# The first head's keys and queries loaded as the last stage of the preparation

## The chip, the cores and the metric

The kernel runs on one core of a Trainium2 chip. The metric is the device time of one launch in microseconds (us). All times of single instructions below come from one profiled execution, and are given as microseconds from the start of its span.

## The reference

The program applies four layers to an input of 4 images of 128 channels by 64 x 64 pixels. Layers 0 and 1 are a state-space block and a convolution, layers 2 and 3 are attention layers with an expert feed-forward each. The change touches the attention of layer 2 alone, which sees an image as L = 4096 tokens of 128 features, that is 16 heads of 8 features:

```python
heads = x.reshape(Bs, Ss, H, D)                  # x is the normed input, H = 16, D = 8
qkv = _qz_ring(heads + rx_theta)                 # products of cosines
q = jnp.transpose(qkv, (0, 2, 1, 3))
scores = jnp.einsum('bhsd,bhtd->bhst', q, q) / np.sqrt(D)
attn = jax.nn.softmax(scores, axis=-1)
ctx = jnp.einsum('bhst,bhtd->bhsd', attn, q)
ctx = jnp.transpose(ctx, (0, 2, 1, 3)).reshape(Bs, Ss, Es)
attn_out = ctx @ w_comb.T + b_comb
x1 = _ln(x + attn_out, g1, beta1)
zf = jnp.cos(x1[..., :NQ_FFN]) * jnp.cos(ry_theta)
h = jax.nn.relu(zf @ w1.T + b1)
ffn_out = h @ w2.T + b2
return _ln(x1 + ffn_out, g2, beta2)              # added to the layer's input by the caller
```

Queries, keys and values are one and the same array q.

## The kernel before

`layer2_attention` runs over the four images b. Activations lie in DRAM (`xd[b]`, 128 features by 4096 tokens). An image has 8 chunks of 512 tokens (`CH`), 32 tiles of 128 tokens. For each b the kernel has two parts:

- **The mixed part.** `prepare(b)` and `feed_forward(b - 1)` are two generators, which `run` advances in turn, a stage each (`in_turns`, L757). Each is a software pipeline over the 8 chunks (`in_turn`, L747): `prepare` has the stages fetch, norm, products and store, `feed_forward` has fetch, attended, first_norm, cosines, hidden, sum_up and last_norm. `prepare` has 4 stages and `feed_forward` 7, so `prepare` runs out first. For b = 0 there is no feed-forward, and after the last image one feed-forward runs alone.
- **The attention.** `attention(b)` goes over the heads h and over blocks of 4 tiles, in steps. In each step PE makes the scores, ACT the exponentials `ex` (4 buffers of a pair of tiles each), DVE transposes (`turned`), POOL sums part of the exponentials (`folded`, `quarters`) and PE weighs the values (`ctx_ps`, `acc_ps`). The order on PE, DVE and POOL is the order in which the code writes it (`manual_schedule`). In the mixed part a scheduler decides the order. Every engine and every DMA queue works through its own list in order, so an entry that waits holds up all behind it.

In `prepare`, the stage `store` copies a chunk's q into `qt` (SBUF) and into `later`, from which `value_d` (DRAM) is written, two chunks at a time for the first three of four block rows. It transposes q, splits it into a high and a low part (`part`) and writes both to `head_d` (DRAM).

In `attention`, `load(h)` (L936) reads one head's keys and queries from `head_d`, 16 DMAs of 64 KB each for the keys and 16 for the queries. Keys read both halves of the tokens of a parity of tiles, queries those of a parity of chunks. `rounded` (L945) casts a loaded tile in place on POOL. The first head is loaded at the start of the attention, on two DMA queues (SP for keys, ACT for queries), and cast at once. The head after it is loaded, on SP alone, while the head before runs. `load_values` (L952) reads a block row's values (`v`, 4 DMAs of 32 KB each) and `spread_values` (L960) multiplies them into `turned_v` on POOL. At the start of the attention two block rows are read and spread.

In `feed_forward`, `fetch` reads a chunk's `den`, `num`, `nrm_in` and `x`; `last_norm` makes the second layer norm (its last instruction is the addition of beta on POOL into `blk`, L120), adds it to `x` on POOL (L1231) and stores to `xd` (L1232).

The pools decide which memory is free when. The mixed part's pool `l2_mid` and the attention's pool `l2_work` follow each other on the same memory, so a tile of the second waits until what lay there before is no longer in use:

```python
with tc.tile_pool(name="l2_big", bufs=1) as big:
    with (
        tc.tile_pool(name="l2_mid", bufs=2) as work,
        ...
    ):
        ...
        run(*parts)
    ...
    with (
        tc.tile_pool(name="l2_work", bufs=2) as work,
        ...
        attention(qt, past, big, work, pssc, psctx, psacc)
```

Of the kernel before, what the change touches and what calls it, by code (L numbers as in the profile page):

```python
# [9 lines left out]
F32 = mybir.dt.float32  # L10
F32R = mybir.dt.float32r
# [6 lines left out]
P = 128  # L18
NB = 4
HW = 64  # L20
L = HW * HW
CH = 512
NCH = L // CH
NTT = L // P
# [750 lines left out]
def layer2_attention(K, xd, dpool, w):  # L775

    nc, tc, mm = K.nc, K.tc, K.mm
# [4 lines left out]
    with ExitStack() as ctx:  # L782
# [50 lines left out]
        den_d = dpool.tile([2, NH, L], F32, name="den_d")  # L833
        nrm_d = [dpool.tile([P, L], F32, name=f"nrm_d{i}") for i in range(2)]

        def prepare(b, big, work, psum):

            n = NTT * NH * (HD + 1)  # L840
            qt = big.tile([P, n + 32], F32, name="qt")
            nc.gpsimd.memset(qt[:, n:], 0.0)
            values = qt[:, 0:n].rearrange("p (h t d) -> p t h d", h=NH, d=HD + 1)
            nc.gpsimd.memset(values[:, :, :, HD : HD + 1], 1.0)
            later = work.tile([P, NH, NTT, HD], F32, name="later", bufs=1)
            shape = [P, 4, NH, HD]
            heads, xs, nrms = {}, {}, {}

            def fetch(c):
                xs[c] = work.tile([P, CH], F32, name="x_in", bufs=3)  # L850
                nc.sync.dma_start(out=xs[c], in_=xd[b][:, c * CH : (c + 1) * CH])

            def norm(c):
                nrms[c] = work.tile([P, CH], F32, name="nrm", bufs=3)
                K.layernorm(nrms[c], xs.pop(c), work, psum)
                nc.sync.dma_start(out=nrm_d[b % 2][:, c * CH : (c + 1) * CH], in_=nrms[c])

            def products(c):

                tp = psum.tile([P, 4, P], F32, name="tok_t", tag="mm")  # L860
                for j in range(4):
                    nc.tensor.transpose(tp[:, j, :], nrms[c][:, j * P : (j + 1) * P], K.ident)
                phi = work.tile(shape, F32, name="phi")
                nc.vector.tensor_tensor(
                    phi.rearrange("p t h d -> p (t h) d"),
                    tp.rearrange("p j (h d) -> p (j h) d", d=HD),
                    theta.unsqueeze(1).to_broadcast([P, 4 * NH, HD]),
                    ALU.add,
                )
                cs = heads[c] = work.tile(shape, F32, name="cs", bufs=3)  # L870
                K.cos(cs, phi, work, shape, "cos")
                cc = lambda d: cs[:, :, :, d : d + 1].rearrange("p t h o -> p (t h) o")
                q0 = work.tile([P, 4 * NH, 1], F32, name="q0")
                nc.gpsimd.tensor_tensor(q0, cc(1), cc(2), ALU.mult)
                for d in range(3, HD):
                    nc.gpsimd.tensor_tensor(q0, q0, cc(d), ALU.mult)
                for d in range(1, HD):
                    nc.vector.tensor_tensor(cc(d), cc(d - 1), cc(d), ALU.mult)
                nc.vector.tensor_copy(cc(0), q0)

            def store(c):

                cs = heads[c]
                nc.scalar.copy(values[:, 4 * c : 4 * c + 4, :, 0:HD], cs)
                nc.gpsimd.tensor_copy(later[:, :, 4 * c : 4 * c + 4].rearrange("p h t d -> p t h d"), cs)
                j = c // 2
                if c % 2 and j < NJ - 1:
                    for q in range(4):
                        nc.sync.dma_start(
                            out=value_d[:, :, j, q].rearrange("h s t d -> s h (t d)"),  # L890
                            in_=later[32 * q : 32 * q + 32, :, BT * j : BT * j + BT].rearrange("s h t d -> s h (t d)"),
                        )
                tp = psum.tile([P, 4, P], F32, name="q_t", tag="mm")
                for j in range(4):
                    nc.tensor.transpose(tp[:, j, :], cs[:, j].rearrange("p h d -> p (h d)"), K.ident)
                tq = work.tile([P, CH], F32, name="tq", tag="phi")
                nc.scalar.copy(tq, tp.rearrange("p j t -> p (j t)"))
                rest = work.tile([P, CH], F32, name="rest", tag="cos_r")
                nc.vector.scalar_tensor_tensor(rest, tq, 4097.0, tq, ALU.mult, ALU.subtract)
                part = work.tile([P, 2, CH], F32, name="part")  # L900
                nc.vector.scalar_tensor_tensor(part[:, 0], tq, 4097.0, rest, ALU.mult, ALU.subtract)
                nc.gpsimd.tensor_tensor(part[:, 1], tq, part[:, 0], ALU.subtract)
                nc.sync.dma_start(
                    out=head_d[:, :, c * CH : (c + 1) * CH].rearrange("z q s -> q z s"), in_=part
                )

            return in_turn(NCH, fetch, norm, products, store), qt

        def attention(qt, dsum, big, work, pssc, psctx, psacc):

# [1 line left out]

            unit = lambda p, c: slice(32 * (2 * p + c), 32 * (2 * p + c) + 32)
            dacc = big.tile([P, NJ - 1, NH, NTT], F32, name="dacc")
            nc.gpsimd.memset(dacc, 0.0)

            def load(h, queues=(nc.sync, nc.sync)):

                out = []
                for keys in (True, False):
                    t = work.tile([P, L // 2], F32R, name="keys" if keys else "queries")
                    raw = t.bitcast(F32)
                    n = P if keys else CH
                    for p in range(2):  # L930
                        for c in range(2):
                            for k in range(4):
                                r = unit(p, c).start + HD * k
                                src = head_d[k // 2 if keys else k % 2, HD * h : HD * h + HD]
                                at = p if keys else c
                                queues[not keys].dma_start(  # L936
                                    out=raw[r : r + HD].rearrange("d (m s) -> d m s", s=n),
                                    in_=src.rearrange("d (m z s) -> d m z s", z=2, s=n)[:, :, at],
                                )
                    out.append(t)  # L940
                return out

            def rounded(t):

                nc.gpsimd.tensor_copy(t, t.bitcast(F32))  # L945

            def load_values(h, j):

# [31 lines left out]
            for n, (h, j, _) in enumerate(steps):  # L980
                begins.setdefault((h, j), n)
                last[h, j] = n
            heads = {0: load(0, (nc.sync, nc.scalar))}
            for t in heads[0]:
                rounded(t)
            values = {(0, 0): spread_values(load_values(0, 0))}
            waiting = []
            order = [(h, j) for h in range(NH) for j in range(NJ - 1)]
# [114 lines left out]
            for n, (h, j, m) in enumerate(steps):  # L1103
                now[0] = n
                keys, queries = heads[h]
                if j in (1, 2) and h + 1 < NH:
                    at = n - begins[h, 1]
                    if at == 0:
                        heads[h + 1] = load(h + 1)
                    if at in (11, 15):  # L1110
                        rounded(heads[h + 1][at == 15])
                while waiting and n >= waiting[0][0]:
# [48 lines left out]
        def feed_forward(b, dsum, work, psum):  # L1161
# [3 lines left out]
            def fetch(c):  # L1165
# [4 lines left out]
                nc.sync.dma_start(out=num, in_=num_d[:, :, cols].rearrange("p q f -> q p f"))  # L1170
                nrm = work.tile([P, CH], F32, name="nrm_in", bufs=4)
                nc.sync.dma_start(out=nrm, in_=nrm_d[b % 2][:, cols])
                x = work.tile([P, CH], F32, name="x", bufs=8)
                nc.sync.dma_start(out=x, in_=xd[b][:, cols])
                loads[c] = x, num, den, nrm

            def attended(c):
                _, num, den, at = loads[c]

                tp = psum.tile([P, 4, 2 * NH], F32, name="den_t", tag="mm")  # L1180
                for j in range(4):
# [15 lines left out]

            def first_norm(c):
                x1 = x1s[c] = work.tile([P, CH], F32, name="x1", bufs=4)
                K.layernorm(x1, loads[c][3], work, psum, g1, beta1)  # L1200

            def cosines(c):
                zp = psum.tile([P, CH], F32, name="z_ps", tag="mm")
# [13 lines left out]
                    nc.scalar.activation(hid[:, k, :], hps[k], AF.Relu, bias=b1[:, k : k + 1])  # L1217

            def sum_up(c):
                hid = hids[c]  # L1220
                fp = psum.tile([P, CH], F32, name="ffn_ps", tag="mm")
                for k in range(4):
                    mm(fp, w2T[:, k, :], hid[:, k, :], start=k == 0, stop=k == 3)
                r = sums[c] = work.tile([P, CH], F32, name="res")
                nc.vector.scalar_tensor_tensor(r, fp, b2, x1s[c], ALU.add, ALU.add)

            def last_norm(c):
                o = work.tile([P, CH], F32, name="blk")
                K.layernorm(o, sums[c], work, psum, g2, beta2)
                x = loads[c][0]  # L1230
                nc.gpsimd.tensor_tensor(x, x, o, ALU.add)  # L1231
                nc.sync.dma_start(out=xd[b][:, c * CH : (c + 1) * CH], in_=x)  # L1232

# [1 line left out]

        past = None
        for b in range(NB + 1):
            with tc.tile_pool(name="l2_big", bufs=1) as big:
                with (
                    tc.tile_pool(name="l2_mid", bufs=2) as work,  # L1240
                    tc.tile_pool(name="l2_ps", bufs=8, space=PSUM) as psum,
                ):
                    parts = [feed_forward(b - 1, past, work, psum)] if b > 0 else []
                    if b < NB:
                        part, qt = prepare(b, big, work, psum)
                        parts.append(part)
                    run(*parts)
                if b == NB:
# [2 lines left out]
                with (  # L1251
# [5 lines left out]
                        engines={mybir.EngineType.PE, mybir.EngineType.DVE, mybir.EngineType.Pool}  # L1257
                    ),
                ):
                    attention(qt, past, big, work, pssc, psctx, psacc)  # L1260


def expert_ffn(K, xs, w, tag):
# [430 lines left out]
```

## Time and profile before

| | us |
|---|---|
| median of 3 runs | 11169.24 (11165.61 to 11181.6) |
| the profiled execution, by the same measure | 11175.99 |
| its span | 11174.1 |

| busy over the span | PE | DVE | ACT | POOL |
|---|---|---|---|---|
| us | 9093.3 | 7817.5 | 7349.5 | 6136.5 |
| share | 81% | 70% | 66% | 55% |

The span falls into layers 0 and 1 (to about 3240), layer 2's attention block (to about 10025, four mixed parts and four attentions, and a last feed-forward) and the rest. Of layer 2 the parts look alike from the second image on:

| stretch | start to end |
|---|---|
| preparation of image 0 | 3235 to 3359 |
| attention of image 0 | 3398 to 4774 |
| feed-forward of 0 with preparation of 1 | 4775 to 5043 |
| attention of image 1 | 5086 to 6460 |
| feed-forward of 1 with preparation of 2 | 6460 to 6730 |
| attention of image 2 | 6772 to 8147 |
| feed-forward of 2 with preparation of 3 | 8147 to 8416 |
| attention of image 3 | 8459 to 9830 |
| feed-forward of 3 | 9830 to 10018 |

How to read the rows of the profile: a group has its line, engine and operation, then output<-input, shapes and count, then busy time and mean duration in ns, then the idle time of the engine just before these instructions with what ended most of it. A row of the timeline has start and duration in us, then engine, line, operation and count, and in brackets the idle time before it and its releaser; neighbouring instructions of one kind are drawn together, so a duration with a count above one spans gaps too. SPq and ACTq are the two DMA queues; their rows tell when transfers are issued, not when they land.

### The profile page before, as it was taken

The numbers are of one execution on the slowest core, as the hardware profiler recorded it, in microseconds if no ns is written. First come the engines' busy times: TensorE is split into PE (matmuls) and PEld (weight loads), VectorE is DVE, ScalarE is ACT, GpSimd is POOL, SyncE is SP. The second block draws the span as 40 slices with busy tenths as digits, with TensorE's granted clock in tenths as the row PEclk, the third lists the DMA queues.
The fourth block names the chain that finished last, engine by engine and source line by source line (L and its number), as shares of the span: only waits on it lengthen the run. The fifth ranks groups of instructions, "written<-read, shape, count | busy, mean of one in ns | idle before, by whom it ended". The sixth has DMA issues, their size and how long they took to land.

```text
span 11174.1 us, 183363 instructions
## 1 busy us (share of the span) xinstructions
PE 9093.3 (81%) x71376; PEld 3383.0 (30%) x71376; DVE 7817.5 (70%) x8718; ACT 7349.5 (66%) x9690; POOL 6136.5 (55%) x3631
## 2 busy tenths in 40 slices
PE   5777777778757999967999967999967999966767
PEld 2222223223122333322333322333322333323433
DVE  2688687687846788856888756878856888844564
ACT  2655454654527899947988947988946998842431
POOL 0466455455626777726777736777736777720000
PEclk8787878878778999978999979999978999978888
DMA  3322322322212221122221222221122221122004
GB/s 86 83 70 52 100 64 62 92 62 61 61 46 39 34 33 34 30 73 36 37 33 32 32 74 34 38 32 33 32 73 34 35 37 33 32 87 78 30 16 136
DMA packets 524324, 581.53 MB, mean 52 GB/s; under 512 B 106232, under 2 KB 329536, under 8 KB 520896
## 3 DMA queue, kind: packets, MB, share of 16 engines
q1 hardware_dynamic: 520896, 565.61, 22.4%
q8 instruction: 563, 9.22, 0.4%
q10 hardware_dynamic: 2560, 4.20, 0.3%
q14 instruction: 305, 2.50, 0.1%
HBM read 373.96 MB, written 76.55 MB: 40 GB/s over the span
## 4 chain that ended last, share of the span: by engine, by line
PE 35%; DVE 16%; DMA 8%; SPq 4%; ACT 3%; issue 2%; POOL 1%; DVEq 0%; ACTq 0%; POOLq 0%
PE ctx_ps L89 12%; PE acc_ps L89 9%; DVE turned L1129 5%; PE score L89 5%; DVE turned L1148 5%; SPq L936 4%; DMA queries<-head_d 3%; DMA keys<-head_d 2%; PE ln_var L89 2%; PE ln_xc L89 1%; PE hid_ps L89 1%; DMA w<-in_L_ffn_weight 1%; PE ffn_ps L89 1%; ACT ex L1142 1%; PE kv L89 1%
## 5 line engine op out<-in xcount | busy, mean ns | idle before, releaser
L1142 ACT ACTIVATE ex<-score 128x1024 f32<-128x1024 f32 x5120 | 4904.7, 1031 | 598.5 <-PE score L89 224.9
L1090 POOL TENSOR_TENSOR folded<-ex 128x1024 f32<-128x1024 f32 x960 | 2291.5, 2387 | 1173.3 <-ACT ex L1142 1141.8
L89 PE MATMUL ctx_ps<-ex,qt 128*32 128x512 f32 x20480 | 2722.5, 596 | 0.0
L1148 DVE STREAM_TRANSPOSE turned<-ex 128x1024 f32<-128x1024 f32 x1536 | 1892.0, 1232 | 596.5 <-ACT ex L1142 392.8
L89 PE MATMUL acc_ps<-turned,turned_v 128*32 128x256 f32 x24576 | 1828.5, 389 | 220.7 <-DVE turned L1129 219.0
L1129 DVE STREAM_TRANSPOSE turned<-ex 128x1024 f32<-128x1024 f32 x1536 | 1854.8, 1208 | 0.0
L89 PE MATMUL score<-queries,keys 32*128 32x512 f32 x10240 | 1360.2, 497 | 240.9 <-POOL queries L945 145.9
L641 DVE TENSOR_TENSOR_SCAN hs<-decay,carry,hs 128x512 f32<-128x512 f32 x1024 | 1247.8, 1263 | 151.6 <-ACT decay L640 142.3
L640 ACT ACTIVATE decay<-dt,a_neg 128x512 f32<-128x512 f32 x1024 | 699.9, 690 | 875.1 <-DVE hs L641 871.5
L1091 POOL TENSOR_TENSOR quarters<-folded 128x512 f32<-128x512 f32 x960 | 1233.8, 1285 | 75.3
L647 POOL TENSOR_TENSOR hs<-hs,c_sb 128x1024 f32<-128x1024 f32 x512 | 1201.7, 2368 | 48.1 <-DMA c_sb<-c_d 28.4
L89 PEld LDWEIGHTS score<-queries,keys 32*128 32x128 f32 x10240 | 523.4, 182 | 2300.9 <-issue 1656.8
L89 PEld LDWEIGHTS acc_ps<-turned,turned_v 128*32 128x32 f32 x24576 | 562.1, 108 | 938.9 <-issue 545.2
L89 PE MATMUL y_ps<-hs,pair 128*64 128x512 f32 x2048 | 654.5, 757 | 223.0 <-POOL hs L647 222.8
L89 PEld LDWEIGHTS ctx_ps<-ex,qt 128*32 128x32 f32 x20480 | 684.9, 110 | 462.2 <-DVE ctx L1072 53.2
L637 DVE TENSOR_TENSOR hs<-dtx,b_ps 128x2048 f32<-128x2048 f32 x256 | 581.4, 2271 | 318.9 <-PE b_ps L89 218.2
L644 POOL COPY carry<-hs 128x4 f32<-128x4 f32 x256 | 65.1, 254 | 1105.2 <-DVE hs L641 1090.8
L1135 DVE TENSOR_REDUCE dacc<-quarters 128x2 f32<-128x512 f32 x960 | 617.2, 648 | 0.0
L1072 DVE COPY ctx<-ctx_ps 128x512 f32<-128x512 f32 x256 | 177.1, 692 | 565.3 <-PE ctx_ps L89 565.3
L89 PE MATMUL ln_var<-ln_sq,mean 128*128 128x512 f32 x448 | 289.6, 732 | 219.0 <-ACT ln_sq L104 183.1
L89 PE MATMUL b_ps<-dbc,spread 32*128 32x512 f32 x512 | 341.6, 751 | 147.8 <-DVE hs L637 147.8
L960 POOL TENSOR_TENSOR turned_v<-v,quarter 128x1024 f32<-128x1024 f32 x192 | 458.9, 2391 | 0.0
(344 smaller groups left out, 9320.8 us busy)
## 6 DMA issues: line engine op xcount, KB each, us to landing
c_sb<-c_d SPq DMA_DIRECT2D x512, 128.0 KB
keys<-head_d SPq DMA_DIRECT2D x1024, 64.0 KB
queries<-head_d SPq DMA_DIRECT2D x960, 64.0 KB
dt<-dt SPq DMA_DIRECT2D x128, 256.0 KB
dtx<-dtx SPq DMA_DIRECT2D x128, 256.0 KB
w<-in_L_ffn_weight SPq DMA_DIRECT2D x32, 1024.0 KB
w<-in_L_ffn_weight SPq DMA_DIRECT2D x128, 256.0 KB
under<-xp SPq DMA_DIRECT2D x384, 66.0 KB
```

The source lines that it names most:

```text
L89: self.nc.tensor.matmul(out, lhsT, rhs, start=start, stop=stop)
L637: nc.vector.tensor_tensor(hs, dtx2, bb.unsqueeze(1).to_broadcast([P, NQ, CH]), ALU.mult)
L640: nc.scalar.activation(ex, dt2[:, q, :], AF.Exp, scale=a_neg[:, q, g : g + 1])
L641: nc.vector.tensor_tensor_scan(hs[:, q, :], ex, hs[:, q, :], carry[:, g, q : q + 1], ALU.mult, ALU.add)
L647: nc.gpsimd.tensor_tensor(at, at, cs.unsqueeze(1).to_broadcast([P, 2, CH]), ALU.mult)
L960: nc.gpsimd.tensor_tensor(t, v.unsqueeze(2).to_broadcast([P, 4 * BT, 4, HD]), quarter.unsqueeze(1).to_broadcast([P, 4 * BT, 4, HD]), ALU.mult,
L1090: nc.gpsimd.tensor_tensor(hs, exs[:, :, 0], exs[:, :, 1], ALU.add)
L1091: nc.gpsimd.tensor_tensor(qs, hs[:, :, 0 : CH // 2], hs[:, :, CH // 2 :], ALU.add)
L1129: nc.vector.transpose(*upright)
L1135: nc.vector.tensor_reduce(at, qs, AX.X, ALU.add)
L1142: nc.scalar.activation(ex, sps[p], AF.Exp, scale=scale, accum_out=dacc[:, j, h, t : t + 1] if summed else None)
L1148: nc.vector.transpose(*upright)
```

## The change

- `load` and `rounded` move out of `attention`, and take the pool as an argument. All loads are now issued on SP.
- A pool `l2_two` of two buffers is opened beside `l2_big`, ahead of `l2_mid`; keys and queries of all heads are allocated in it.
- `prepare` gets a last stage, behind its pipeline: it loads head 0 and casts it. The mixed part's scheduler orders these instructions. `attention` receives the loaded head.
- To make room in `l2_mid`, `later` holds two chunks rather than all eight (one buffer), and its copies of the last two chunks, which nothing read, are left out. `x` of the feed-forward has 3 buffers for 8, and is read in `sum_up`, one stage ahead of its use, rather than in `fetch`.

```diff
-        def prepare(b, big, work, psum):
+        def load(h, keep_in):
+            out = []
+            for keys in (True, False):
+                t = keep_in.tile([P, L // 2], F32R, name="keys" if keys else "queries")
...
+                            nc.sync.dma_start(
...
+        def prepare(b, big, two, work, psum):
...
-            later = work.tile([P, NH, NTT, HD], F32, name="later", bufs=1)
...
-                nc.gpsimd.tensor_copy(later[:, :, 4 * c : 4 * c + 4].rearrange("p h t d -> p t h d"), cs)
                 j = c // 2
+                if c % 2 == 0 and j < NJ - 1:
+                    laters[j] = work.tile([P, NH, BT, HD], F32, name="later", bufs=1)
+                if j < NJ - 1:
+                    at = laters[j][:, :, 4 * (c % 2) : 4 * (c % 2) + 4]
+                    nc.gpsimd.tensor_copy(at.rearrange("p h t d -> p t h d"), cs)
...
-            return in_turn(NCH, fetch, norm, products, store), qt
+            first = []
+
+            def stages():
+                yield from in_turn(NCH, fetch, norm, products, store)
+                first.extend(load(0, two))
+                for t in first:
+                    rounded(t)
+                yield
+
+            return stages(), qt, first
...
-                    t = work.tile([P, L // 2], F32R, name="keys" if keys else "queries")
...
-            heads = {0: load(0, (nc.sync, nc.scalar))}
-            for t in heads[0]:
-                rounded(t)
+            heads = {0: first}
...
-                        heads[h + 1] = load(h + 1)
+                        heads[h + 1] = load(h + 1, two)
...
-                x = work.tile([P, CH], F32, name="x", bufs=8)
-                nc.sync.dma_start(out=x, in_=xd[b][:, cols])
-                loads[c] = x, num, den, nrm
+                loads[c] = num, den, nrm
...
             def sum_up(c):
+                x = loads[c] = work.tile([P, CH], F32, name="x", bufs=3)
+                nc.sync.dma_start(out=x, in_=xd[b][:, c * CH : (c + 1) * CH])
...
-            with tc.tile_pool(name="l2_big", bufs=1) as big:
+            with (
+                tc.tile_pool(name="l2_big", bufs=1) as big,
+                tc.tile_pool(name="l2_two", bufs=2) as two,
+            ):
```

## The prediction

> **What bounds the kernel now.** I read the page's groups first, for who waits, then the table of stretches over layer 2, then the timeline at one boundary. In the groups (busy, mean ns of one, then idle time before and its releaser) the score matmuls own a wait that no later matmul has:
>
> ```profile
> L89 PE MATMUL score<-queries,keys 32*128 32x512 f32 x10240 | 1360.2, 497 | 240.9 <-POOL queries L945 145.9
> ```
>
> The table of stretches (start:end, length, busy time of PE, PEld, DVE, ACT, POOL, granted clock, DMA share, GB/s) shows where it falls:
>
> ```profile
> 3360.00:3400.00 40.00, 1.80 (x6) 1.17 (x6) 0.00 (x0) 1.87 (x2) 5.59 (x3) 0.50 0.53 76
> 3400.00:4775.00 1375.00, 1302.10 (x14589) 464.53 (x14586) 1104.48 (x1169) 1230.01 (x1568) 1046.18 (x561) 1.00 0.20 32
> 4775.00:5045.00 270.00, 163.12 (x416) 71.61 (x416) 146.53 (x288) 115.27 (x171) 80.44 (x98) 0.75 0.25 78
> 5045.00:5088.00 43.00, 1.68 (x6) 1.16 (x6) 0.00 (x0) 1.74 (x2) 5.46 (x3) 0.50 0.53 61
> ```
>
> Attention (1375 us) holds PE busy 95% of it; a microsecond lost at its start has nothing to be recovered from later. Before each attention stand some 40 us in which no compute engine works. The timeline of the second boundary (start, length, engine, line) says what fills it:
>
> ```profile
> 5042.23 1.26 POOL L1231 TENSOR_TENSOR x<-x,blk 128x512 f32<-128x512 f32 x1
> 5045.59 28.35 SPq L936 DMA_DIRECT2D keys<-head_d  x16
> 5045.61 29.44 ACTq L936 DMA_DIRECT2D queries<-head_d  x16
> 5075.08 1.28 ACT L1142 ACT_TABLE_LOAD   x1 [36.49 <-DMA keys<-head_d]
> 5076.58 7.37 SPq L952 DMA_DIRECT2D v<-value_d  x8
> 5082.54 1.89 POOL L945 CAST keys<-keys 128x2048 fp32r<-128x2048 f32 x1 [39.05 <-DMA keys<-head_d]
> 5084.37 1.90 POOL L945 CAST queries<-queries 128x2048 fp32r<-128x2048 f32 x1
> 5086.23 4.68 POOL L960 TENSOR_TENSOR turned_v<-v,quarter 128x1024 f32<-128x1024 f32 x2
> ...
> 5087.54 3.77 ACT L1142 ACTIVATE ex<-score 128x1024 f32<-128x1024 f32 x4 [11.18 <-PE score L89]
> ...
> 5090.86 2.38 POOL L1090 TENSOR_TENSOR folded<-ex 128x1024 f32<-128x1024 f32 x1
> ```
>
> The feed-forward's last addition ends at 5043.49, its store lands about 2.1 us later and frees the pool, and only then do the 32 loads start, since their tiles lie in a pool on the same memory. They land 37 us later, are cast, and the first exponential runs 44.05 us after the feed-forward's end (43.50 and 44.03 at the third and fourth boundary: 6729.67 to 6773.17, 8415.85 to 8459.88). The data was ready long before: the last head_d store is issued by 4962.7, the first of the last six xd stores at 4981:
>
> ```profile
> 4948.05 14.69 SPq L903 DMA_DIRECT2D head_d<-part  x2
> 4980.99 62.84 SPq L1232 DMA_DIRECT2D xd<-x  x6
> ```
>
> **What the skill says.** The Trainium skill, *DMA: Bandwidth & Descriptors*, "Issuing engines are not separate DMA queues": issuing on two engines saves only sequencer time. The trace agrees: 32 loads on two queues took 29.5 us to issue, and those of head 1 on SP alone 11.18 + 14.70 = 25.9. The same page, "Anatomy of one DMA": a semaphore wait sits on the issuing sequencer, and a fixed cost of about 2 us is mostly the receipt; here last addition to first load is 2.1, 2.4 and 2.1 us. Its "Rules for kernel authors" advise an early DMA with a late wait, which is what the new placing is. *ScalarE: Activation LUTs*, "What ACT_TABLE_LOAD costs", gives 1283 ns; the trace shows 1.28 us, at present hidden behind the loads.
>
> **The change, part by part.** In the order of the built programs PE and DVE stand as before, instruction for instruction, and ACT too, but that it loses its 64 DMA issues. Only SP and POOL change. On POOL, second boundary, the end of the feed-forward reads:
>
> ```
> x+=blk (chunk 4); cast keys; blk 5; blk 6; cast queries; x+=blk 5; blk 7; x+=blk 6; x+=blk 7; turned_v x2; folded
> ```
>
> *1. The loads, moved to SP.* 3 wait for the even chunks alone and go ahead of the last head_d store; 1 + 16 + 12 follow it, then three xd stores, and x loads. Store at 4962.4 plus 2.6 us (3359.5 to 3362.1 at the first boundary) gives 4965; 16 keys at 0.70 us and 13 queries at 0.92 (head 1's pace) make 23.2 us, so 4988 for the last issue and, 7.4 us after (first boundary: last key load issued 3387.0, cast 3394.4), 4996 for landing. The keys' cast has its place at 5016.8, behind the addition of chunk 4: 21 us of room. Cover: the feed-forward's last five chunks. Cost 0; if the cover goes, one for one.
>
> *2. What SP queues behind them.* The xd store of chunk 2 is ready at 4981 and goes at 4988; no engine waits for it but x's load of chunk 5. That and chunks 6 and 7 wait for the stores of chunks 2, 3, 4; the last is made at 5016.8, lands by 5019, the loads by about 5023. Chunk 5's addition is at 5029. Cost 0, room 6 us. The slot waits of chunks 3 and 4 (2.1 us each) hold SP while its next entry, a head_d or nrm_d store, is not due: 0; at worst 2 x 2.1 x 3 boundaries = 13 us.
>
> *3. The casts on POOL.* Keys: in a 10.9 us idle stretch, 0. Queries (1.90): ahead of chunk 5's addition, from 5034.9 on, pushing the last addition from 5043.49 to 5044.66: 1.17 us each.
>
> *4. The new start.* Score matmuls need only PSUM, free by about 5041. The exponentials' buffers lie on the old pool, so ACT's table load waits for the last xd store to land: 5044.66 + 2.1 + 1.28 = 5048.1 against 5087.54. Gains: 44.05 - 4.55 = 39.5; 43.50 - 4.84 = 38.7; 44.03 - 4.55 = 39.5. **Sum 117.7 us.**
>
> *5. What is late next: the values.* The v loads are still in attention's pool: issued from about 5045.5, eight in 3.4 us (0.42 the median) to 7.4 (at this boundary), landed about 2.3 us after; two multiplications of 2.35 on POOL, in front of the first fold. Fold starts 6.3 to 9.8 us after the first exponential, against 3.3 now. Four ex buffers let ACT run on; at the first boundary an exponential waits for a fold only from the ninth pair (0.35 us), so there is about 1 us of slack: loss 2 to 5.3, I take 3.5 each: **-10.5.** POOL has some room in these steps (two folds of 3.67 us in four steps of 2.29), so the lag dies out, but PE's lost time stays.
>
> *6. The first boundary* has no feed-forward to hide under. 30 loads follow the last head_d store: 16 x 0.70 + 14 x 0.92 = 24.1 us from 3362.1, landed by 3392.6 to 3393.6, one cast left of two: score at 3394.6 instead of 3398.2. **+3.6** (0 to 7).
>
> *7. x's loads moved out of the start* of four feed-forwards: three of 256 KB (0.45 us of SP each) no longer stand among the first loads. **+4** in all (-4 to +8). *8. `later`* loses its copies of the last two chunks (2 x 0.61 us of POOL, beside idle time) and gets one buffer of two chunks, whose next use is 13 us or more after its stores are issued: 0. Head 1 and later load as before.
>
> Sum: 117.7 - 10.5 + 3.6 + 4 = 114.8 us. The profiled execution took 11175.99 (span 11174.1), so 11061 by its measure; the median of the runs, 11169.24, lies 6.8 lower, and 11169.24 - 114.8 = **11054.5, say 11055**.
>
> **The rivals.** *A: the values take the wait over.* If v lands as late after issue as the keys do (7.4 us) with the issues at 7.4, folds start 16 us after the exponentials and some 12 are lost each time: gain 89, 11080. For it: v goes on a queue full of head 1's keys. Against: the v loads stand ahead of most of them. *B: nothing is gained*, since the new pool's tiles or the exponentials wait for something I don't see: 11165. Against: the order has no such wait. *C, slower: the casts hold the feed-forward up.* Chunks 5 to 7 stand behind the queries' cast; loads that land after 5035 delay the end one for one. The gain of 39 is gone at 5077 (2.5 us of idle POOL before chunk 7's blk are used up first), 112 us after their start, that is 2.1 MB at 19 GB/s. Were only 16 GB/s left to them, 131 us, they would land at 5096 and the exponentials start at 5107, 19 us later than now: three times that, 58, with part 5's 10.5 and less the 7.6 of parts 6 and 7, is 61, and 11230. Against: the stretch moves 78 GB/s at a DMA share of 0.25, and alone the loads get 61 GB/s.
>
> **How the numbers follow.** 0.2% (22 us) is about what can be told from no change. As summed 0.76, own range 11040 to 11072; A 0.16; B 0.03; C 0.05. Faster 0.92, same 0.03, slower 0.05. The low end takes parts 5, 6, 7 at their best (loss 6, +7, +8: gain 127) and a few us for the boundary, 11037; the high end takes in A and 12 us of SP waits beside it, 11096.
>
> **What would show it.** Right: head 0's loads lie inside the feed-forward, landing 20 us before the keys' cast; ACT's table load about 3 us after the last addition; first exponentials near 5048 on this clock, shifted by the first boundary; the stretches of feed-forward still 270 us, those of attention about 1378. Wrong in part 1 or 2: POOL waits for queries or x inside the feed-forward, which grows past 272. Wrong in part 5: folds over 10 us behind the first exponential. The prediction fails if less than 75 us is gained.

## The result, and the profile after

| us | before | after |
|---|---|---|
| median | 11175.07 (11165.61 to 11181.6, 4 runs, three of them those above) | 11057.91 (11046.44 to 11065.94, 4 runs) |
| profiled execution, its span | 11175.99, 11174.1 | 11065.94, 11064.2 |

The ratio is 0.9896 [0.988, 0.9912], that is 116 us less (98 to 134); the changed kernel is about 1% faster. The prediction was 11055 (11037 to 11096).

In the page's groups the row of the score matmuls (columns as before) has lost the wait that it was chosen for: 124.5 us of idle time instead of 240.9, and POOL's cast of the queries no longer ends most of it (it still does at the first boundary, 40 us).

```profile
L89 PE MATMUL score<-queries,keys 32*128 32x512 f32 x10240 | 1358.8, 497 | 124.5 <-ACT ex L1153 74.7
```

The table of stretches of the changed kernel, with the first boundary, the first attention, the second mixed part and the second boundary:

```profile
3369.00:3408.00 39.00, 1.58 (x6) 1.07 (x6) 0.00 (x0) 1.67 (x2) 6.66 (x4) 0.50 0.53 77
3408.00:4778.00 1370.00, 1300.69 (x14568) 463.56 (x14572) 1101.20 (x1167) 1230.21 (x1568) 1044.76 (x557) 1.00 0.20 32
4778.00:5050.50 272.50, 163.93 (x444) 72.43 (x436) 149.70 (x290) 115.12 (x171) 83.36 (x99) 0.76 0.30 85
5050.50:5054.00 3.50, 0.00 (x0) 0.00 (x0) 0.00 (x0) 1.28 (x1) 0.00 (x0) 0.50 0.37 122
```

The second boundary is 3.5 us long where 43 us stood, and holds nothing but ACT's table load. The mixed part in front of it moves 85 GB/s at a DMA share of 0.30, instead of 78 at 0.25: the head's loads are in there now. The first boundary is as long as ever. The timeline of the second boundary, the answer to the prediction's:

```profile
4971.31 11.08 SPq L853 DMA_DIRECT2D keys<-head_d  x16
4982.65 10.82 SPq L853 DMA_DIRECT2D queries<-head_d  x12
4993.70 29.09 SPq L1243 DMA_DIRECT2D xd<-x  x3
...
5022.38 1.89 POOL L862 CAST keys<-keys 128x2048 fp32r<-128x2048 f32 x1
5023.60 1.37 SPq L1230 DMA_DIRECT2D x<-xd  x3
...
5040.54 1.89 POOL L862 CAST queries<-queries 128x2048 fp32r<-128x2048 f32 x1
5042.39 1.26 POOL L1242 TENSOR_TENSOR x<-x,blk 128x512 f32<-128x512 f32 x1
...
5047.84 2.48 POOL L1242 TENSOR_TENSOR x<-x,blk 128x512 f32<-128x512 f32 x2
...
5052.48 3.57 SPq L965 DMA_DIRECT2D v<-value_d  x8
5052.71 1.28 ACT L1153 ACT_TABLE_LOAD   x1 [8.46 <-DMA xd<-x]
5054.00 3.77 ACT L1153 ACTIVATE ex<-score 128x1024 f32<-128x1024 f32 x4
...
5055.81 4.70 POOL L973 TENSOR_TENSOR turned_v<-v,quarter 128x1024 f32<-128x1024 f32 x2 [5.50 <-DMA v<-value_d]
5060.47 2.38 POOL L1101 TENSOR_TENSOR folded<-ex 128x1024 f32<-128x1024 f32 x1
```

The last load is issued at 4982.65 + 10.82 = 4993.47, 29 us ahead of the keys' cast. Neither cast has a bracket, so POOL waits for no load. The bracket of the table load says that ACT waits for the feed-forward's last store, which is the prediction's part 4. The bracket of `turned_v` says that the values are what is late next, its part 5.

The ledger, from the same events in both traces (the first layer-2 load of `x_in`, the last addition to `part`, first and last exponential, last addition to `x`):

| us | before | after | difference |
|---|---|---|---|
| preparation of image 0, and from there to the first exponential | 123.39 + 40.32 | 123.79 + 39.08 | -0.84 |
| last addition to first exponential, boundaries 2 to 4 | 44.05, 43.50, 44.03 | 3.68, 3.56, 3.68 | -120.66 |
| three mixed parts | 274.49, 271.78, 275.15 | 272.64, 271.90, 273.18 | -3.70 |
| last feed-forward | 186.30 | 188.83 | +2.53 |
| four attentions | 1369.59, 1370.35, 1367.53, 1370.29 | 1370.07, 1369.96, 1368.16, 1369.83 | +0.26 |
| layer 2 | 6780.77 | 6658.36 | -122.4 |
| the rest of the span | | | +12.4 |

The rest is code that the change doesn't touch: layer 2 began at 3235.70 before, at 3244.74 after, and at anything from 3230.55 to 3248.60 in the experiments. So kernels are compared below by layer 2 and its parts. Two executions of the changed kernel differed by 14 us in layer 2 (6658.36 and 6644.36), spread over all its parts but the three later boundaries, which repeat to 0.1 us. A part's few microseconds in one execution are therefore no finding, unless they repeat at each boundary. This holds above all for experiments 3 to 8, which were executed once each.

### The profile page after: what moved, and what is told of

Read it like the earlier page. It is cut to its first block, busy times and chain, and to the rows that moved or that the text cites. A ratio compares the mean times of both kernels' runs of the same rounds, so it can differ in the third digit from the quotient of the medians.

```text
span 11064.2 us, 183405 instructions
## 1 busy us (share of the span) xinstructions
PE 9097.1 (82%) x71376; PEld 3379.2 (31%) x71376; DVE 7816.5 (71%) x8718; ACT 7349.4 (66%) x9690; POOL 6134.3 (55%) x3623
## 3 DMA queue, kind: packets, MB, share of 16 engines
q1 hardware_dynamic: 523456, 569.81, 22.2%
## 5 line engine op out<-in xcount | busy, mean ns | idle before, releaser
L89 PE MATMUL score<-queries,keys 32*128 32x512 f32 x10240 | 1358.8, 497 | 124.5 <-ACT ex L1153 74.7
```

What stands on the lines that cost most here:

```text
L89: self.nc.tensor.matmul(out, lhsT, rhs, start=start, stop=stop)
```

## The experiments

**1. The room alone.** The kernel before with the small `later` and the late `x`, but head 0 loaded in the attention, on two queues.

```diff
# against the kernel before
-            later = work.tile([P, NH, NTT, HD], F32, name="later", bufs=1)
+                    laters[j] = work.tile([P, NH, BT, HD], F32, name="later", bufs=1)
...
-                x = work.tile([P, CH], F32, name="x", bufs=8)          # in fetch
+                x = loads[c] = work.tile([P, CH], F32, name="x", bufs=3)   # in sum_up
```

> The kernel before, with only the edits that make room: later of two chunks, x with 3 buffers read in sum_up. My theory: the gain is the three hidden loads, and the room is worth nothing by itself. The boundaries keep their 43.5 to 44.1 us from last addition to first exponential, the mixed parts change by -1 to -3 us each (x is no longer among the first loads), the last feed-forward by +-2.5; total within 10 us of before, ratio 0.999 to 1.001. Rival: part of the 117 us gained comes from x's later reads, by 20 us or more: ratio 0.998 or below.

Measured: 11174.64 (12 runs) beside 11170.56 (15 runs of the kernel before), ratio 1.0002 [0.9994, 1.0011]. The later boundaries stay at 44.19, 41.45 and 44.47. The room itself brings nothing that 12 runs show (the interval is -7 to +12 us); the gain is the loads' place.

**2. The pool alone.** The changed kernel, but the loads and casts are written where `attention` begins, into the early pool.

```diff
                 yield from in_turn(NCH, fetch, norm, products, store)
-                first.extend(load(0, two))
-                for t in first:
-                    rounded(t)
                 yield
...
-            heads = {0: first}
+            heads = {0: load(0, two)}
+            for t in heads[0]:
+                rounded(t)
```

> The changed kernel, but head 0's loads and casts are written where they were, at the start of the attention; the pool still opens early. The scheduler can then move the loads up, since no memory holds them back, but places them behind the feed-forward's own transfers: in the built order 16 keys and 5 queries stand between the xd stores, and the last 7 queries behind the last of them. Theory A (the queue's order counts): those 7 are issued at about the time of the last store and land some 12 us later, the queries' cast follows, and each of the three boundaries has its first exponential 10 to 13 us later than in the changed kernel, so 14 to 17 us after the last addition instead of 3.7; total about 11094. Theory B (the pool alone counts, where the stage is written is nothing): 11058. Theory C (the early stage alone counts): as before, 11175.

Measured: 11083.67 (11070.69 to 11093.62, 4 runs), ratio 0.9918 [0.9901, 0.9935]; boundaries of 13.76, 14.03 and 13.62. The scheduler does move the loads into the feed-forward once their tiles are free, though the code has them later: three quarters of the gain come with the pool, without the stage (90 of 121 us at the three boundaries). What is left lies in SP's order, as the timeline of its second boundary shows:

```profile
5046.92 0.33 SPq L1242 DMA_DIRECT2D xd<-x  x1
5047.29 4.82 SPq L853 DMA_DIRECT2D queries<-head_d  x7
5052.28 4.18 SPq L962 DMA_DIRECT2D v<-value_d  x8
5056.30 1.89 POOL L862 CAST queries<-queries 128x2048 fp32r<-128x2048 f32 x1 [9.40 <-DMA v<-value_d]
```

Seven of the queries' loads stand behind the feed-forward's last store on the in-order queue, and the cast waits until 5056.30 (the release is put down to v, but the cast reads the queries, whose last issue was at about 5052.1). The stage in `prepare` is what ranks them ahead of the stores.

**3. Three times the loads.** Each of head 0's 32 loads is made three times, into the same tile.

```diff
-                for p in range(2):
+                for p in [p for _ in range(times) for p in range(2)]:
...
-                first.extend(load(0, two))
+                first.extend(load(0, two, 3))
```

> The changed kernel with head 0 loaded three times over into the same tiles, 96 DMAs for 32, to find how much the feed-forward hides. At the first boundary, with no cover, the 64 more cost their full time, 64 x 0.80 = 51 us. At the other three they land at about 5052 on the changed kernel's clock instead of 5001; the queries' cast stands ahead of the last three additions on POOL, where it now runs at 5040.5, and the xd stores and x loads stand behind the loads on SP. Theory (cover of 39 us, then one for one): the last addition ends 9 to 12 us later, and so does the first exponential: 41 of 51 us are hidden each time, total near 11058 + 51 + 30 = 11139. Rival (the added transfers disturb the feed-forward as they run, so nothing is really free): the mixed parts grow by 25 us or more each, total over 11185.

Measured: 11109.73. At the first boundary, where nothing covers them, the 64 further loads cost 45.3 us (84.42 for 39.08). In the mixed parts they cost +4.9, -0.2 and +5.6 (277.54, 271.70, 278.77), less than the 9 to 12 of the theory, and the boundaries stay at 3.70, 3.57, 3.70. In the timeline of its second mixed part:

```profile
5006.37 42.78 SPq L853 DMA_DIRECT2D keys<-head_d  x48
5049.45 32.28 SPq L853 DMA_DIRECT2D queries<-head_d  x44
...
5075.48 1.89 POOL L862 CAST keys<-keys 128x2048 fp32r<-128x2048 f32 x1
5084.66 1.90 POOL L862 CAST queries<-queries 128x2048 fp32r<-128x2048 f32 x1 [7.29 <-DMA xd<-x]
```

These 92 loads of 64 KB took 75.4 us to issue beside the feed-forward (5006.37 to 5081.73), 80 GB/s. Alone, at the first boundary, 93 took 73.5 us (3364.88 to 3438.39), 83 GB/s. Rival C needed 19 GB/s or less beside the feed-forward; the runs give four times that. Most of three times the traffic is covered, and here the cover ends: POOL waits 7.29 us ahead of the queries' cast, whose last load is issued at 5081.73 (the release is put down to the store of `x`). In this build the keys' cast also stands later in POOL's order, behind `blk` of chunks 5 and 6, so the cover isn't measured in an unaltered order.

**4. Later folds.** The first two multiplications of the values are made four times, or twice, so that POOL reaches the first fold later.

```diff
-                nc.gpsimd.tensor_tensor(t, ...)
+                for _ in range(times):
+                    nc.gpsimd.tensor_tensor(t, ...)
...
-            values = {(0, 0): spread_values(load_values(0, 0))}
+            values = {(0, 0): spread_values(load_values(0, 0), 4)}    # or 2; and for order[1]
```

> The changed kernel with the two multiplications of values at the start of each attention done four times each, 6 more of 2.35 us, so 14.1 us more of POOL ahead of the first fold. The prediction's rule (an exponential waits for a fold as soon as the lag passes about 1 us): the first copy of ctx_ps, which stands 38.9 us after the first exponential in the changed kernel, moves by about 14 us, and so does the attention's end: 4 x 14 = 56 us in all. What the trace of the changed kernel hints (3.2 us of lag moved that copy by -0.7 us, and before ACT idled 2.8 and 0.8 us at 28 to 31 us): some 4 to 6 us of the lag are absorbed within the first block, the rest counts: the copy moves by 8 to 10 us, the total by 32 to 40.

> The changed kernel with the first two multiplications of the values made twice instead of four times, so that the first fold is some 4.7 us later instead of 14.6: at the three later boundaries some 11.2 us after the first exponential. The prediction's rule (each microsecond of lateness past about 1 holds up the exponentials) says that each attention is 4.7 longer, 19 in all: 11077. The rule read from four times (up to some 7.7 us cost nothing, then one for one) says that the first ctx copy comes some 42.4 after the first exponential and each later attention is 3.5 longer, the first one (fold at 6.8) unchanged: some 10 to 11 in all, 11068. If the free lateness is larger than 11 at any boundary, nothing is seen there.

Measured, from the first exponential to the first fold (the lag) and to the first ctx copy, attention 0 and then the mean of attentions 1 to 3:

| us | lag | first ctx copy | length of the attention |
|---|---|---|---|
| after | 2.10; 6.59 | 39.15; 39.04 | 1370.07; 1369.32 |
| twice | 7.00; 11.42 | 42.80; 42.69 | 1372.10; 1371.94 |
| four times | 16.73; 21.19 | 52.61; 52.41 | 1383.36; 1383.01 |

At boundaries 2 to 4 a lag of 11.42 costs 3.65 up to the first ctx copy, and one of 21.19 costs 13.37: in both the first 7.8 us are free, and the rest counts one for one. At the first boundary 7.00 costs 3.65 and 16.73 costs 13.46: there only 3.3 us are free. The expectation for twice took attention 0 to have the room of the others, and missed there. (The times were 11052.61 for twice and 11087.45 for four times; layer 2 took 6661.90 and 6696.12.) ACT's timeline with four times says where the room lies, at the first boundary and then at the second:

```profile
3402.63 1.94 ACT L1154 ACTIVATE ex<-score 128x1024 f32<-128x1024 f32 x2 [0.47 <-PE score L89]
3414.47 1.94 ACT L1154 ACTIVATE ex<-score 128x1024 f32<-128x1024 f32 x2 [9.89 <-POOL folded L1102]
...
5058.55 5.61 ACT L1154 ACTIVATE ex<-score 128x1024 f32<-128x1024 f32 x6 [0.17 <-PE score L89]
5075.06 1.02 ACT L1154 ACTIVATE ex<-score 128x1024 f32<-128x1024 f32 x1 [10.91 <-POOL folded L1102]
```

At the first boundary ACT runs 8 exponentials, four steps, before it waits for a fold; at the second it runs 12, six steps. Two steps at 2.3 us are about the 4.5 us between 3.3 and 7.8. A step is two exponentials, and there are four buffers of a step each in both cases; what differs is which exponential has to wait. By the code the first, second, fifth and sixth step are folded, the third and fourth are not. At the first boundary the 9th and 11th exponential (steps 5 and 6) wait for the first and the second fold. At the second the 13th and 15th do (steps 7 and 8; their waits are 10.91 and 1.67), and with twice the 11th (2.83). That fits buffers that aren't handed out in turn: there step 5, or steps 5 and 6, take those of steps 3 and 4, which no fold reads. The traces hold no addresses, so this is inferred.

The changed kernel has an assignment of its own. In its third attention, at a lag of 6.76, it is the 9th exponential that waits:

```profile
6708.59 4.84 ACT L1153 ACTIVATE ex<-score 128x1024 f32<-128x1024 f32 x5 [0.23 <-POOL folded L1101]
```

So about 6.5 us are free in the changed kernel's later attentions (6.76 less 0.23, an estimate), and its lag just fits; the 7.8 belongs to kernels whose folds are later. At boundaries 2 to 4 the first exponential that waits for a fold is a later one in the builds with later folds: the 9th at a lag of 6.76, the 11th at 11.31, the 13th at 21.11. At the first boundary it is the 9th even at 16.73. Why the builds differ so isn't shown.

**5. Earlier values.** The first two blocks of values are loaded in the preparation's last stage, into the early pool, which the later blocks use too; the multiplications stay.

```diff
+                for at in ((0, 0), (0, 1)):
+                    first.append(load_values(*at, two))
                 yield
```

> The changed kernel with the first two block rows' value loads also issued in the preparation's last stage, into the early pool; their multiplications stay at the attention's start. The first fold then stands some 3 us after the first exponential at boundaries two to four, as before the change, instead of 6.5. The prediction's part 5 (10.5 us lost to late values): each attention ends 3.5 us sooner against its first exponential, 10.5 us in all. What spread_4 showed (a lag of up to some 7.7 us costs nothing at these boundaries, then one for one): first ctx copy 38.9 to 39.2 us after the first exponential as it is, attention 1370, gain 0.

Measured: 11059.23. The lag falls from 6.5 to 3.2 at the later boundaries, and the attentions last 1369.22, 1369.73, 1369.25 and 1369.71, as before. Part 5's wait is real, and costs nothing that shows.

**6. The table ahead of time.** An exponential of one column on the last chunk of the feed-forward (and of image 0's preparation), so that ACT's table is there when the buffers come free.

```diff
+                if c == NCH - 1:
+                    tiny = work.tile([P, 1], F32, name="tiny", bufs=1)
+                    nc.scalar.activation(tiny, o[:, 0:1], AF.Exp)
                 nc.gpsimd.tensor_tensor(x, x, o, ALU.add)
```

> The changed kernel with one exponential of a single column behind the last layer norm of each feed-forward, and behind the last chunk of image 0's preparation, so that ACT's table is loaded while the last store lands or the loads run. Theory: the table load now waits for what the exponential waits for, and adds its 1.28 us to each boundary. Expected: from last addition to first exponential 2.4 us instead of 3.7, first boundary 37.8 instead of 39.1 (give or take the 5 us by which its loads differ from run to run); layer 2 shorter by 5 us. Rival: the table load overlaps the wait for the store in hardware anyway, or ACT is not what the first exponential waits for: nothing changes.

Measured: 11039.76; boundaries of 2.41, 2.29 and 2.40, so 1.28 us less at each. In its timeline the first exponential now waits for the store directly:

```profile
5026.35 0.20 ACT L1247 ACTIVATE tiny<-blk 128x1 f32<-128x1 f32 x1 [2.35 <-POOL blk L120]
...
5031.17 3.77 ACT L1156 ACTIVATE ex<-score 128x1024 f32<-128x1024 f32 x4 [4.62 <-DMA xd<-x]
```

Its first boundary took 32.96, but that is not all the table: the 13 last query loads took 10.29 us to issue here, 12.68 in the changed kernel and 11.26 in its second profile, with nothing else on their way. The pace moves this boundary: the kernel of experiment 4 with four times, whose 13 loads took 10.17 us, has 33.89 there without the early table.

**7. Split loads.** Three quarters of each load after chunk 5 of the preparation, the last quarter at its end, in all four preparations.

```diff
+            def stored(c):
+                store(c)
+                if c == NCH - 3:
+                    first.extend(load(0, two, hi=3))
...
-                first.extend(load(0, two))
+                load(0, two, first, 3, 4)
```

> The changed kernel with head 0's loads in two portions: three quarters of the tokens behind chunk 5's store, the last quarter behind chunk 7's, 64 DMAs for 32. Theory (the first boundary is bound by issuing and landing what follows the last store): 32 DMAs of 16 KB at 0.3 to 0.4 us each replace 30 of 64 KB at 0.8, so the stretch from the last part to the first exponential shrinks from 39 to 23 to 27 us; the other boundaries stay at 3.7 us and the mixed parts within 3 us, for the loads are hidden there either way. Layer 2 shorter by 12 to 16 us. Rival (a DMA's fixed cost, not its size, sets the pace): the stretch stays at 36 us or more.

Measured: 11043.29. The first boundary fell to 19.49, further than expected. The mixed parts took 276.96, 276.79 and 277.25, some 4.4 us more each than in the changed kernel; which of the further issues cost that isn't shown.

**8. The queries on ACT's queue again,** in their new place.

```diff
-                            nc.sync.dma_start(
+                            (nc.scalar if h == 0 and not keys else nc.sync).dma_start(
```

> The changed kernel with head 0's queries issued on ACT's queue, as before the change, while the keys stay on SP. The prediction took the move to SP alone as worth 0[...]. Theory: the first boundary stays within 3 us; in the three mixed parts ACT now has 16 issues of 0.7 to 1.7 us in its own list, between the feed-forward's activations, so each part gets 5 to 20 us longer and the move to SP is what spares this. Rival: ACT is idle over half of the part and takes the issues for nothing: mixed parts within 3 us.

Measured: 11085.53. The three mixed parts last 291.43, 281.85 and 288.53, together 44 us more than the changed kernel's; the later boundaries stay (3.49 to 3.64), and the first one, at 37.61, is within what it varies by. ACT's timeline in the second mixed part:

```profile
4965.80 21.25 ACTq L853 DMA_DIRECT2D queries<-head_d  x13
4987.15 0.60 ACT L104 ACTIVATE ln_sq<-ln_xc 128x512 f32<-128x512 f32 x1 [21.04 <-DMA queries<-head_d]
```

13 issues take 21.25 us of ACT's own in-order list, and the layer norm behind them waits 21.04. The two queues bring nothing for it: SP's 16 keys take 24.70 us at the same time (4967.37 to 4992.07), so 29 loads need 26.3 us from ACT's first on, while SP alone issued 28 in 22.2 (4971.31 to 4993.47).

**9. The version that came out,** and the changed kernel beside it on one chip: the early table at each boundary, the split for image 0 alone. The cut is against experiments 6 and 7 taken together.

```diff
-                if c == NCH - 3:
+                if b == 0 and c == NCH - 3:
...
-                load(0, two, first, 3, 4)
+                if b == 0:
+                    load(0, two, first, 3, 4)
+                else:
+                    first.extend(load(0, two))
```

> The changed kernel with the two edits that paid: the exponentials' table is fetched by a one-column exponential on the last chunk ahead of each attention, and the loads of image 0 alone are split (three quarters of them after chunk 5 of the preparation, the last quarter at its end). The other three preparations load in one piece, since the split cost them some 4 us each. If the two gains add: the three later boundaries last 2.4 us instead of 3.7, the first one some 18 instead of 39, the mixed parts are those of the changed kernel (270 to 274), and layer 2 is shorter by 21 + 4 = 25 us: 11033 beside 11058, with 11027 to 11042 as bounds. If the split's cost in the mixed parts was only chance, the same. If the extra issues on SP in preparation 0 hold up its stores, that preparation (123.8) becomes longer by some us and the gain is 20 or less.

> The changed kernel unaltered, run beside the version above on one chip, so that the two are compared on the same ground: 11058 (11046 to 11066) and boundaries of 3.7 us again.

Measured: 11035.32 (11024.62 to 11036.93), ratio to the kernel before 0.9875 [0.9859, 0.9892]; the changed kernel 11053.31 (11035.02 to 11062.36), 0.9889 [0.9874, 0.9904]; the kernel before 11170.84. The medians are 18 apart, 25 were expected, and the two intervals overlap, so the total alone doesn't prove it. The parts do: the first boundary takes 18.20 instead of 35.33, the later ones 2.40, 2.29 and 2.50 instead of 3.68, 3.56 and 3.67, and the mixed parts are alike (269.25, 272.67, 273.01 beside 269.24, 272.91, 272.41). 17.1 and 3.7 make 20.9; the missing 4 are the reference, whose first boundary was 35.33 this time instead of 39.08. Layer 2 took 6627.25 instead of 6644.36. The lag at the later boundaries is 7.70 to 8.06 here, since the first exponential comes earlier and the values don't; that is about the 7.8 that experiment 4 found free, so little room for late values is left. In the timeline of this version's first boundary the second, short set of loads is what remains to be waited for:

```profile
3368.13 5.78 SPq L854 DMA_DIRECT2D keys<-head_d  x16
3373.95 4.69 SPq L854 DMA_DIRECT2D queries<-head_d  x14
...
3380.27 1.89 POOL L863 CAST queries<-queries 128x2048 fp32r<-128x2048 f32 x1 [2.84 <-DMA v<-value_d]
...
3383.45 3.77 ACT L1165 ACTIVATE ex<-score 128x1024 f32<-128x1024 f32 x4 [19.53 <-DMA v<-value_d]
```

Both releases are put down to `v`, but the cast reads the queries, whose last load is issued at 3378.64, and the exponential reads the scores made from them.

## Why the prediction was right

The likeliest case happened, with its mechanism, and its sum of 114.8 stands against 122.4 in layer 2 and 116 between the medians. Step by step:

- **Part 1, the loads under the feed-forward at no cost: right.** Their queue order, their pace (11.08 us for 16 keys, 0.69 each; 10.82 for 12 queries, 0.90 each) and the unhindered casts came as worked out. Experiment 3 shows that the cover was far larger than the 21 us that the prediction counted on: some 53 us more of loads cost 5.6 us at most. What the part left out is that the move to SP matters: it took from the skill's section "Issuing engines are not separate DMA queues" (*DMA: Bandwidth & Descriptors*) that a second engine saves sequencer time alone, and gave no price to the time that ACT's own list would have lost. Experiment 8 prices the choice at 44 us. The section says that issuing from several engines saves sequencer time, "usually small relative to the DMA itself"; here that time is the point, since it stands in a compute engine's list. At the old place ACT had nothing to do while it issued; inside the feed-forward it has.
- **Part 2, SP's queue: right.** The `x` loads go out at 5023.60 and POOL's addition of chunk 5 (5042.39) doesn't wait for them; none of the 13 us at worst came.
- **Part 3, the queries' cast: right.** It stands right ahead of chunk 5's addition, and pushes the last addition by 1.18 us, as predicted (1.17).
- **Part 4, the new start: right.** Predicted 3.38 us from the last addition (2.1 for the store's landing, 1.28 for the table), measured 3.68, 3.56 and 3.68. From the end of the last addition at 5050.32 to the table load are 2.39 us. The fixed cost of some 2 us that the prediction took from the skill (*DMA: Bandwidth & Descriptors*, "Anatomy of one DMA") is stated there for DMAs that GpSimd issues; the store goes out on SP, so the measured 2.1 to 2.4 us is what counts here. With the push counted, 117.1 us for 117.7.
- **Part 5, the values late: mechanism right, price wrong.** The lag came at 6.47 to 6.76, inside the 6.3 to 9.8. Of the loss of 10.5 nothing shows: the four attentions are 0.26 us longer together, where the changed kernel's two profiles differ by 3.9, and experiment 5, which takes the lag away, doesn't shorten them. The term that failed is "about 1 us of slack". The wait of 0.35 us at the ninth pair, from which it was read, doesn't measure slack: the changed kernel's first attention has 0.34 there at a lag of 2.10. And it was carried from the first boundary to the other three, where the buffers are handed out otherwise: experiment 4 finds 3.3 us free at the first, and in the changed kernel's later attentions a lag of 6.76 makes ACT wait 0.23.
- **Part 6, the first boundary: not settled by one trace.** Scores started 2.5 us sooner after the last `part`, predicted 3.6; but ACT's table load, hidden behind the loads in the rows that the prediction read, is in the open here, and 1.24 was left. In the timeline of the changed kernel's first boundary it starts only after the scores:

```profile
3403.23 1.90 POOL L862 CAST queries<-queries 128x2048 fp32r<-128x2048 f32 x1 [10.02 <-DMA v<-value_d]
...
3405.18 1.58 PE L89 MATMUL score<-queries,keys 32*128 32x512 f32 x6 [40.17 <-POOL queries L862]
3406.32 1.28 ACT L1153 ACT_TABLE_LOAD   x1 [40.63 <-PE score L89]
```

  The table load's 1.28 us is the step that the part left out. The size can't be told from one trace: the loads' pace from execution to execution moves the boundary by more than this term. It took 39.08, 35.33, 37.10, 33.89, 38.15 and 38.88 us in the six traces with these 30 loads behind the last store (the changed kernel twice, experiment 4 twice, 5 and 2), 37.1 on average, and 40.33 and 41.81 in the two with the loads in the attention (before and experiment 1). That is 3 to 5 us less, so the 3.6 may well be right on average.
- **Part 7, x's loads: not told apart.** With the pushes of part 3, mixed parts and last feed-forward were to be 0.5 shorter, and are 1.2 shorter, within what two executions differ by. **Part 8** fits: experiment 1, which holds both, is at 1.0002.

The rivals: B is out. A's wait for the values was seen, but at a lag of 6.6 us and not 16, with the eight loads issued in 3.57 us and not 7.4, and it cost nothing that shows. C asked for loads that crawl beside the feed-forward; they kept 80 GB/s there (experiment 3).

The two terms whose size was off, a loss of 10.5 that didn't come (part 5) and a gain of 3.6 of which 1.2 came (part 6), are together the 8 us between 114.8 and the 122.4 of layer 2 in these two traces. The interval of the medians (98 to 134) can't tell these two sums apart. That the 116 us between the medians come within 2 us of the sum is luck: the two misses go opposite ways, and the untouched rest of the span differs by 12 us between the traces.

## What to carry to other kernels

When a stage begins with loads whose data is long in memory, look at what holds the tile, not the data: a pool opened ahead of the stage before lets the loads run under it, and a place in the writing order ahead of that stage's stores lets them pass on an in-order queue. Issue such loads from an engine that computes nothing in that stretch. Slack that is read at one boundary isn't the slack of the next, nor that of the next build: ask at each which step waits for the late one, and measure by making it later, as experiment 4 does.

## What the runs showed of the hardware

- In the changed kernel the table load takes over the wait of the activation behind it: it starts when that activation could (at the first boundary after the scores, at the others after the last store), so its 1.28 us is in the open. In the kernel before it stood behind ACT's own DMA issues and ran ahead of the scores. It takes 1.28 us in every trace here. An activation of one column ahead of the wait, 0.20 us, takes it out (experiment 6).
- Loads of 64 KB on two queues at once take 1.54 us (SP) and 1.63 us (ACT) each to issue, against 0.69 and 0.90 on SP alone. The sum is no faster (29 loads in 26.3 us, against 28 in 22.2), and the issuing engine's list is held: a layer norm waited 21.04 us behind 13 issues on ACT (experiment 8).
- The same 13 loads on the same queue, with no compute engine at work, took 10.17 to 12.68 us to issue in seven traces of six kernels.
